# Two tiles of a shared expert moved: one behind the first attention projection, one into the first sums stage

## The chip, the cores and the metric

The kernel runs on one core of a Trainium2 chip. The metric is the device time of one execution in microseconds; a lower time is better. Time before: median 1554.01 us of three runs.

## What is computed

The reference is one block in three parts on x of 4 x 512 tokens, 512 wide, in float32:

```python
x = x + 0.5 * ffn(layernorm(x))        # router, 64 experts of 192, top 6, and a shared expert
x = x + attn(layernorm(x))             # 16 heads of 32, rope; attn adds its own input again
x = x + 0.5 * ffn(layernorm(x))
```

The shared expert is `silu(x @ ws_gate) * (x @ ws_up) @ ws_down`, for every token. In attn, scores of a head are 512 x 512, then softmax, then the product with the values, then the output projection.

## The kernel before, in words

Tokens are handled in 16 tiles of 128, four tiles to a batch (B = 4 batches, TPB = 4 tiles). The first feed-forward layer routes all tokens, computes the shared expert of the first three batches between the steps of the routing, and then runs the 64 routed experts (`experts`, L519), whose outputs are added into two arrays in HBM, `total[0][0]` and `total[0][1]`, by scattering DMAs from GpSimd (L576). Attention follows batch by batch, and the last feed-forward layer after it.

The join lies between the first experts and the attention (L1041 to L1053). There the shared expert of the fourth batch is still to be done; its four input tiles stay in SBUF in `xs[B - 1]`. For each tile it has these steps, all of class `Route`:

- `gate` (L477, by way of `gate_up`, L204): 4 matmuls of 128x384 on TensorE (gate and up together, L208), a tanh on ScalarE (L211), and, unless it is told to leave it out, `product`: two operations on VectorE (L214, L215).
- `turn_h` (L494): two transposes on TensorE (L201) and a copy on ScalarE to `hT` (L202).
- `down` (L502): two matmuls of 128x512 (L508), and an add into the tile of x on VectorE (L509).

The trace counts two TensorE records to each of these float32 matmuls and, for a transpose of this kind, one.

`load` (L603) brings each batch's tiles of x together: for batch 0 it loads the tile and a second operand, `odd`, on SyncE's queue (L608, L613), and the row adds them on VectorE (L786). For batches 1 and 2 it loads the tile and lets GpSimd accumulate the other array into it by DMA (L616); for batch 3 GpSimd accumulates both arrays into the tiles in SBUF.

`qkv(b)` (L780) gives the projections of a batch as a list of pieces, each with a cost written by hand: `row(0)` 0.1 and `turn(0)` 0.5, then for each tile `proj(i, 0)`, `proj(i, 1)`, `turn(i + 1)`, `proj(i, 2)` and two `heads`; a projection is marked 3.4. `row(i)` is a chain of some 18 operations on VectorE (add, statistics, reciprocal root by iteration, the layer norm itself at L799 and L800); `row(1)` is called inside `proj(0, 0)`, and the loads of batches 1 to 3 are issued inside `row(1)`. `turn` transposes the normed tile and copies it to `lT` on ScalarE. At the join the first batch's pieces run one after the other.

`sums(b, ...)` (L933) goes over the scores once to get maxima and sums. It has 16 rows (4 head groups c by 4 query tiles q). A row has its scores on TensorE (L965, two of three buffers of PSUM), two maxima on VectorE (L968) and four exponentials in place on ScalarE (L973). Pieces of other work are taken between, with these two methods of `Pieces`:

```python
    def short(self):

        if self.left and self.left[0][0] < 1.0:
            self.take()

    def long(self, keep=0):

        if sum(p[0] >= 1.0 for p in self.left) > keep:
            self.short()
            self.take()
```

A row issues its scores and maxima, then calls `short()`, then issues its exponentials, then calls `long(2)`. So a piece under 1.0 at the head of the list comes ahead of the row's exponentials, and a longer one behind them, and the last two long pieces are left for the end of the stage. In the first sums stage the list is the second batch's `qkv(1)`: with 12 projections, rows 1 to 10 take one each.

Each engine works its own queue in order. From the attention on, the order on TensorE, ScalarE and VectorE is the order in which the code issues; GpSimd's and SyncE's queues are ordered by the scheduler. The tile `sg` and the tile `hT` of the shared expert have one buffer each.

Of the kernel before, what the change touches and what calls it, by code (L numbers as in the profile page):

```python
# [18 lines left out]
B, S, D = 4, 512, 512  # L19
T = B * S  # L20
NT = T // P
TPB = S // P
# [61 lines left out]
def macaron_kernel(ctx: ExitStack, tc: tile.TileContext, X, ln_w, ln_b, W_in, W_out, gate_w, bias,  # L84
# [543 lines left out]
    with ExitStack() as s:  # L628
# [4 lines left out]
        with ExitStack() as f:  # L633
            rp = f.enter_context(tc.tile_pool(name="rp0", bufs=2))
            f.enter_context(tc.manual_schedule(engines={mybir.EngineType.SP}))
            xs = []
            for t in range(NT):
                g, i = divmod(t, TPB)
# [9 lines left out]
            route0 = route = Route(0)  # L648
# [4 lines left out]
            for t in range(2 * TPB + 1):  # L653
                g, i = divmod(t, TPB)
# [73 lines left out]
    with ExitStack() as s:  # L728
# [6 lines left out]
        psT = s.enter_context(tc.tile_pool(name="psT", bufs=2, space=bass.MemoryType.PSUM))  # L735
# [13 lines left out]
        xs, stats, qT, kT, v, nmT, keyed = xas, {}, {}, {}, {}, {}, {}  # L749
        work = Pieces()  # L750
# [103 lines left out]
        def project(b):  # L854
            mv = small.tile([P, TPB, 2], F32, tag="mv4", name="mv")

            def part(q):
                po = psT.tile([P, 512], F32, tag="ps", name="po")
                for c in range(NC):
                    nc.tensor.matmul(po, lhsT=qT[b][:, c, q * P:(q + 1) * P], rhs=win[3][:, c, :],  # L860
                                     start=c == 0, stop=c == NC - 1)
                nc.vector.tensor_add(xs[b][q], xs[b][q], po)
                if b < B - 1:
                    stat_later(b, mv, q)
                    if q == TPB - 1:
                        steps_later(route.ready(b, mv))
            return [(3.4, lambda q=q: part(q)) for q in range(TPB)]
# [173 lines left out]
        pieces, following = qkv(0), qkv(1)  # L1041
        pieces.insert(-2, following.pop(0))
        odds = [load(0, i, op) for i in range(2)]
        route0.use(rp, psT, Banks(), 1)
        for i in range(TPB + 1):
            if i < TPB:
                route0.gate(B - 1, i)
            if i == TPB:
                pieces.pop(0)[1]()
            if i > 0:  # L1050
                route0.turn_h(B - 1, i - 1)
                route0.down(B - 1, xs[B - 1], i - 1, False)
        nc.vector.memset(nmq, 0.0)  # L1053
        places(0)
        places(1)
# [2 lines left out]
        while work.left:  # L1058
# [2 lines left out]
            if done == len(pieces) // 3:  # L1061
                summed(1)
            work.flush(1)
        work.add(following)

        for ins in clear(1, range(NT + 1)):
            tc.add_manual_dep(ins, keyed[0].name, SENT, reason="behind the loads of the sums")
# [1 line left out]
        for b in range(B):  # L1069
            if b > 0:  # L1070
                pieces = project(b - 1)
                if b + 1 < B:
                    places(b + 1)
                    following = qkv(b + 1)
# [26 lines left out]
    with ExitStack() as s:  # L1101
# [6 lines left out]
        with ExitStack() as f:  # L1108
            g = B - 1
# [75 lines left out]
```

## Time and profile before

| what | value |
|---|---|
| timed runs | 1554.78, 1554.01, 1548.78 us; median 1554.01 |
| profiled execution | 1560.13 us |
| its span | 1558.4 us |
| mean granted TensorE clock | 0.946 |
| last expert's matmuls end (TensorE) | 451.0 us |
| shared expert of the fourth batch on TensorE | 452.41 to 474.35 us |
| first projection starts | 480.15 us |
| first sums stage: first scores, last scores | 532.98, 605.71 us |
| first scores of the context stage behind it | 617.51 us |

The profiled execution is one run; its span is from its first to its last instruction. In the rows of a timeline the columns are the start in us from the span's start, the duration in us, the engine (PE is TensorE, PEld its weight loads, DVE VectorE, ACT ScalarE, POOL GpSimd, SP SyncE), the line, the operation, what it writes and reads, shapes and the number of merged instructions, and in brackets the engine's idle time before it with what ended it. A row of the table of stretches has the stretch, its length, busy time and count for TensorE, its weight loads, VectorE, ScalarE and GpSimd, then the granted TensorE clock (1.00 is full), the busy share of the DMA engines and GB/s. On the page, the numbers behind an engine are its busy us, its share of the span and its instructions.

### The profile page before, as it was taken

What the parts mean: (1) busy time and instruction counts of PE and PEld (TensorE: products, weight loads), DVE (VectorE), ACT (ScalarE), POOL (GpSimd) and SP (SyncE); (2) the same over time, 40 slices, a digit from 0 to 9 for tenths busy, and PEclk for the clock granted to TensorE, in tenths of its full rate; (3) what the DMA queues carried; (4) which work ended last, traced back from release to release, by engine and by line L of the source; (5) the groups of instructions that cost most, each with busy time, mean ns of one, the idle gap of its engine ahead of it and who ended that gap; (6) DMA issues with size and microseconds to landing.
All of it is one profiled execution on the core that took longest, in us unless ns stands there. A gap on an engine that the chain in (4) does not pass through costs nothing.

```text
span 1558.4 us, 23015 instructions
## 1 busy us (share of the span) xinstructions
PE 1400.1 (90%) x9024; PEld 802.0 (51%) x9024; DVE 625.6 (40%) x1572; ACT 594.6 (38%) x1161; POOL 350.7 (23%) x321
## 2 busy tenths in 40 slices
PE   4785999999998998999999999988998799999990
PEld 4553777776753443333443434335334577777660
DVE  7575222211216575267245842375416422222210
ACT  4431121211111487668635774566452112121120
POOL 2001355554435000000000000000000245555535
PEclk9898899999999997999999999996898899999995
DMA  5477699999999300000000020000006389999989
GB/s 196 144 230 257 184 336 333 328 335 336 341 276 179 115 9 1 1 1 1 28 24 8 1 74 21 4 28 27 24 1 246 118 282 339 337 333 335 329 248 123
DMA packets 127035, 254.57 MB, mean 163 GB/s; under 512 B 15800, under 2 KB 32312, under 8 KB 126928
## 3 DMA queue, kind: packets, MB, share of 16 engines
q1 hardware_dynamic: 87216, 192.96, 35.2%
q0 software_dynamic: 39424, 59.97, 18.0%
q8 instruction: 72, 1.18, 0.3%
q14 instruction: 35, 0.29, 0.1%
q10 hardware_dynamic: 288, 0.16, 0.0%
HBM read 202.21 MB, written 56.95 MB: 166 GB/s over the span
## 4 chain that ended last, share of the span: by engine, by line
PE 56%; ACT 5%; DVE 4%; DMA 2%; issue 2%; POOL 1%; another core or an unknown queue 0%; POOLq 0%; SPq 0%; DVEq 0%; ACTq 0%
PE pq L811 10%; PE gu L549 6%; PE sct L995 5%; PE sc L965 4%; PE cx L1018 4%; PE sct L999 4%; PE ps_t L201 4%; PE eo L568 3%; PE po L860 3%; PE gu L208 3%; PE gu L553 2%; PE so L508 2%; PE eo L571 2%; ACT sc L973 2%; DMA w<-in_L_ffn_w_up_dram 1%
## 5 line engine op out<-in xcount | busy, mean ns | idle before, releaser
L526 POOL DMA_INDIRECT xr<-xn_d,en x128 | 119.5, 934 | 887.3 <-DVE sg L215 716.1
L549 PE MATMUL gu<-bT,w 128*128 128x96 f32 x2048 | 245.5, 278 | 8.3 <-DMA w<-in_L_ffn_w_up_dram 8.3
L549 PEld LDWEIGHTS gu<-bT,w 128*128 128x128 f32 x2048 | 238.5, 195 | 11.6 <-issue 11.5
L973 ACT ACTIVATE sc<-sc,nmq 128x512 f32<-128x512 f32 x256 | 168.9, 660 | 55.7 <-DVE nmq L968 50.0
L811 PE MATMUL pq<-w,lT 128*128 128x512 f32 x384 | 179.6, 615 | 6.6 <-ACT lT L202 2.7
L968 DVE TENSOR_REDUCE nmq<-sc 128x2 f32<-128x1024 f32 x128 | 151.5, 1221 | 74.0 <-PE sc L965 73.8
L576 POOL DMA_INDIRECT total<-ob,en x96 | 138.6, 1443 | 156.3 <-ACT ob L575 120.7
L575 ACT ACTIVATE ob<-eo,xr 96x512 f32<-96x512 f32 x128 | 80.5, 678 | 183.5 <-PE eo L571 180.2
L560 DVE SCALAR_TENSOR_TENSOR sg<-sg,gu 128x288 f32<-128x288 f32 x64 | 29.1, 454 | 301.7 <-ACT sg L559 224.0
L1006 ACT ACTIVATE pT<-sct 128x1024 f32<-128x1024 f32 x128 | 124.1, 1022 | 63.6 <-PE sct L999 63.6
L559 ACT ACTIVATE sg<-gu 128x288 f32<-128x288 f32 x64 | 26.2, 410 | 318.0 <-PE gu L555 318.0
L568 PE MATMUL eo<-w,hT 128*96 128x512 f32 x256 | 125.3, 612 | 0.0
L202 DVE COPY bT<-ps_t 128x384 f32<-128x384 f32 x128 | 65.7, 553 | 144.0 <-PE ps_t L201 121.1
L811 PEld LDWEIGHTS pq<-w,lT 128*128 128x128 f32 x384 | 71.6, 195 | 97.5 <-issue 80.9
L965 PE MATMUL sc<-kT,qT 32*128 32x512 f32 x512 | 93.8, 697 | 8.5 <-ACT sc L973 7.8
L555 PE MATMUL gu<-bT,w 128*64 128x96 f32 x1024 | 98.2, 249 | 0.0
L553 PE MATMUL gu<-bT,w 128*64 128x96 f32 x1024 | 98.2, 249 | 0.0
L995 PE MATMUL sct<-qT,kT 32*128 32x512 f32 x512 | 94.5, 658 | 2.3 <-ACT pT L1006 2.3
L208 PE MATMUL gu<-wsgu,xT 128*128 128x384 f32 x256 | 95.1, 519 | 1.4 <-ACT ob L575 1.4
L553 PEld LDWEIGHTS gu<-bT,w 128*64 128x64 f32 x1024 | 86.2, 137 | 6.0
L999 PE MATMUL sct<-nmT,pick 4*128 4x512 f32 x512 | 88.9, 612 | 0.0
L555 PEld LDWEIGHTS gu<-bT,w 128*64 128x64 f32 x1024 | 86.2, 137 | 0.0
(162 smaller groups left out, 1642.6 us busy)
## 6 DMA issues: line engine op xcount, KB each, us to landing
w<-in_L_ffn_w_gate_dram SPq DMA_DIRECT2D x64, 768.0 KB
w<-in_L_ffn_w_up_dram SPq DMA_DIRECT2D x64, 768.0 KB
w<-in_L_ffn_w_down_dram SPq DMA_DIRECT2D x64, 768.0 KB
total<-zero SPq DMA_DIRECT2D x39, 256.0 KB
xn_d<-xn SPq DMA_DIRECT2D x32, 256.0 KB
x<-in_L_attn_X_dram SPq DMA_DIRECT2D x16, 256.0 KB
x<-total POOLq DMA_DIRECT2D x16, 256.0 KB
out_dram<-x SPq DMA_DIRECT2D x16, 256.0 KB
```

Source lines behind the costliest of these rows:

```text
L208: nc.tensor.matmul(gu[:rows, :2 * F].rearrange("p (w f) -> p w f", w=2), lhsT=bT[:, c, :], rhs=weights[:, :, c, :], start=c == 0, stop=c = ...
L549: nc.tensor.matmul(g[:, k, :], lhsT=w[:, k, c, f:f + P], rhs=x[:, c, :], start=c == 0, stop=c == DC - 1)
L553: nc.tensor.matmul(g[:FC, 2, :], lhsT=w[:, 0, c, P:F], rhs=xa[:, c, :], start=c == 0, stop=c == DC - 1)
L555: nc.tensor.matmul(g[FC:, 2, :], lhsT=w[:, 1, c, 0:FC], rhs=xb[:, c, :], start=c == 0, stop=c == DC - 1)
L568: nc.tensor.matmul(eos[k][:CAP], lhsT=hT[:, k, :], rhs=wd[:, 2 * k, :], start=True, stop=False)
L576: nc.gpsimd.indirect_dma_start(out=total[layer][k], in_=ob, in_offset=None, out_offset=bass.IndirectOffsetOnAxis(ap=en[:, e:e + 1], axis=0 ...
L811: nc.tensor.matmul(pq, lhsT=lTs[i][:, c, :], rhs=win[n][:, c, :], start=c == 0, stop=c == DC - 1)
L965: nc.tensor.matmul(scs[j // 2][:, j % 2, :], lhsT=qT[b][rows, c, q * P:(q + 1) * P], rhs=kT[b][rows, c, :], start=True, stop=True)
L968: nc.vector.tensor_reduce(nmv[:, q, 2 * pair:2 * pair + 2, c], scs[pair], AX.X, ALU.max, negate=True)
L973: nc.scalar.activation(scs[j // 2][:, j % 2, :], scs[j // 2][:, j % 2, :], AF.Exp, bias=nmq[:, q, j * DH + c:j * DH + c + 1], accum_out=sm ...
L995: nc.tensor.matmul(scs[j // 2][:, j % 2, :], lhsT=kT[b][rows, c, kt * P:(kt + 1) * P], rhs=qT[b][rows, c, :], start=True, stop=False)
L999: nc.tensor.matmul(scs[j // 2][:, j % 2, :], lhsT=pick[rows, c, :], rhs=nmT[b][c // (NC - 1)][rows, :], start=False, stop=True)
```

## The change

At the join the loop over the four tiles is written out for three. The gates of tiles 0, 1 and 2 are issued, with tile 2's product left out for then; tiles 0 and 1 are turned and brought down. Then comes the first row's chain on VectorE (`pieces.pop(0)`), and behind it tile 2's product. Tile 2's turn and down are one piece of 1.7, put behind `proj(0, 0)`. Tile 3 becomes two long pieces in the list of the first sums stage, two entries ahead of its last projection: its gates with product (3.1), for which the PSUM pool is set to that of the transposes and projections, and its turn and down (1.7).

In the built program the order on TensorE changes in these places alone. The gates of tile 3 stand in row 10 of the first sums stage, its turn and down behind the scores of row 11 and ahead of those of row 12, and the projection that row 10 had stands behind the scores of row 12. On ScalarE the tanh of tile 3 comes ahead of row 11's exponentials, and the copy to `hT` behind them. On VectorE tile 3's product is ahead of row 11's maxima and its add ahead of row 12's. On GpSimd the accumulations into the tiles 2 and 3 of the fourth batch come first among those of L616 instead of last. Line numbers from the join on are higher by 12, and behind the first list of the sums stage by 13.

```diff
         route0.use(rp, psT, Banks(), 1)
-        for i in range(TPB + 1):
-            if i < TPB:
-                route0.gate(B - 1, i)
-            if i == TPB:
-                pieces.pop(0)[1]()
+
+        g, own = B - 1, xs[B - 1]
+        for i in range(3):
+            route0.gate(g, i, None if i < 2 else 1)
             if i > 0:
-                route0.turn_h(B - 1, i - 1)
-                route0.down(B - 1, xs[B - 1], i - 1, False)
+                route0.turn_h(g, i - 1)
+                route0.down(g, own, i - 1, False)
+        pieces.pop(0)[1]()
+        route0.product(g, 2)
+
+        def third():
+            route0.turn_h(g, 2)
+            route0.down(g, own, 2, False)
+
+        def fourth():
+            route0.turn_h(g, 3)
+            route0.down(g, own, 3, False)
+
+        pieces.insert(2, (1.7, third))
+        fourths = [(3.1, lambda: (setattr(route0, 'psM', psT), route0.gate(g, 3))), (1.7, fourth)]
...
-        work.add(following)
+        at = max(k for k, p in enumerate(following) if p[0] > 3.0)
+        work.add(following[:at - 2] + fourths + following[at - 2:])
```

## The prediction

> **What bounds the kernel now.** I read the page first, then the timeline of TensorE with VectorE from 440 to 535 us (the join of the first experts with the first attention row), then the timelines of TensorE, ScalarE and VectorE from 574 to 632 us (the end of the first sums stage), the granted clock in short windows, the moved bytes in 2 us windows, and how the changed program orders its instructions on each engine. On the page TensorE is busy 90% of the span and holds 56% of the chain that ended last:
>
> ```profile
> PE 1400.1 (90%) x9024; PEld 802.0 (51%) x9024; DVE 625.6 (40%) x1572; ACT 594.6 (38%) x1161; POOL 350.7 (23%) x321
> ```
>
> So a move can only win where TensorE idles. The join has such a place:
>
> ```profile
> 466.01 2.75 PE L208 MATMUL gu<-wsgu,xT 128*128 128x384 f32 x8
> ...
> 468.59 0.38 PE L201 MATMUL ps_t<-ident,sg 128*96 128x128 f32 x2
> ...
> 472.28 0.68 DVE L786 TENSOR_TENSOR x<-x,odd 128x512 f32<-128x512 f32 x1
> ...
> 477.54 0.75 DVE L800 SCALAR_TENSOR_TENSOR ln<-ln,rs,lnb_b 128x512 f32<-128x512 f32 x1
> ...
> 478.39 1.08 PE L201 MATMUL ps_t<-ident,ln 128*128 128x128 f32 x4 [4.04 <-issue]
> 480.15 9.16 PE L811 MATMUL pq<-w,lT 128*128 128x512 f32 x16 [0.67 <-ACT lT L202]
> ```
>
> VectorE adds the third tile's product at 471.67 and only then starts the first row's chain of small operations (472.28 to 478.29, 6.0 us). TensorE has finished the fourth tile's product by 474.35 and waits 4.04 us. From 480 to 586 us it runs with gaps of 0.25 to 0.7 us. Then the sums stage runs out of projections:
>
> ```profile
> 582.91 3.70 PE L811 MATMUL pq<-w,lT 128*128 128x512 f32 x8 [0.25 <-ACT qT L835]
> 586.54 1.99 PE L965 MATMUL sc<-kT,qT 32*128 32x512 f32 x12
> 590.61 1.13 PE L965 MATMUL sc<-kT,qT 32*128 32x512 f32 x4 [2.09 <-ACT sc L973]
> 592.09 1.13 PE L965 MATMUL sc<-kT,qT 32*128 32x512 f32 x4 [0.35 <-ACT sc L973]
> 594.20 8.71 PE L965 MATMUL sc<-kT,qT 32*128 32x512 f32 x20 [0.98 <-ACT sc L973]
> ```
>
> Numbering the sixteen rows of this stage by their scores (8 records each), row 10 has the last projection and rows 11 to 15 are paced by ScalarE's exponentials (L973), four to a row, 3.07 us with their accumulator reads. The first of rows 11, 12 and 13 start so:
>
> ```profile
> 588.97 0.66 ACT L973 ACTIVATE sc<-sc,nmq 128x512 f32<-128x512 f32 x1 [1.32 <-DVE nmq L968]
> ...
> 592.56 0.66 ACT L973 ACTIVATE sc<-sc,nmq 128x512 f32<-128x512 f32 x1 [0.52 <-DVE nmq L968]
> ...
> 595.53 0.65 ACT L973 ACTIVATE sc<-sc,nmq 128x512 f32<-128x512 f32 x1
> ```
>
> **The change, part by part.** No operation is added or dropped: the third tile's gates, product, turn and down and the fourth's are each issued once in both programs. SyncE's queue keeps its order.
>
> *Earlier first row.* VectorE now meets that chain right after the second tile's add, which ends at 466.90, if the two operands have landed. The hardware queue moved 0.49 MB from 462 to 464 and 0.47 MB from 464 to 466; the second operand is the third load of 0.262 MB, so its last bytes move near 465.3. The ninth load (2.36 MB) moved its last bytes near 471.4 and its waiter on GpSimd started at 473.58, 2.1 us later; by that measure the operand is there at 467.4. I take 467.4: 472.28 - 467.4 = 4.9 us earlier for everything that follows. Bounds: 466.9 (5.4) and 472.28, when it was used without a wait (0). What fell out of TensorE's queue was cover for this chain: it now idles from 466.2 to about 473.5, 7.3 instead of 4.04 us. Its clock then starts at half, as it did before (0.50 from 478 to 484), so the first projection costs the same.
>
> *Third tile behind the first projection.* Turn and down now lie between the two first projections. From the rows of before: turn 0.43, then ScalarE copies the projection (0.58) and only then hT, so the down starts about 1.0 after the projection's end (0.67 of waiting in the old place), and lasts 1.82. The second projection starts 2.8 to 3.1 later: +3.0 us. Its product (0.70) and the second row's chain on VectorE (5.7) lie beside 7 us of projection and cost nothing.
>
> *The add that now waits for DMA.* In the changed program GpSimd issues the accumulations into the third and fourth tiles first, ahead of the adds, so VectorE's add of the third tile (L509) waits for two of them. The first can go at 463.2; by the queue's progress (0.27 MB done by 472, sharing with the loads) it lands near 473.6, the second is issued then, and one alone takes some 5.7 us (issued near 495.6, its waiter on GpSimd starts at 501.30), 7.5 behind a full queue: there at 479 to 482. VectorE reaches the add near 484, when the down ends. Behind the add stand the rotation of the second projection (its copy comes at 488) and the third row's chain, with 3 us to spare. Cost 0; a landing after 491 would cost its lateness one for one. The second row batch's accumulations in the same queue go from 473.6 to about 478 to 488; their statistics are read from 490 on. Cost 0. One statistic moves ahead of the third row's chain, so the 0.45 us wait of the fourth turn (515.17) should go: -0.4.
>
> *Fourth tile in the sums stage.* Row 10 gets the gates (2.58) instead of the projection, row 11 turn and down, row 12 the projection. By busy time this looks free: TensorE idles some 9 us in rows 11 to 15, and ScalarE gets only 0.33 + 0.37. The order says otherwise. A row of the fourth batch's sums shows the gate's product ahead of a row's maxima:
>
> ```profile
> 1034.23 0.35 DVE L214 SCALAR_TENSOR_TENSOR sg<-sg,gu 128x192 f32<-128x192 f32 x1 [2.00 <-ACT sg L211]
> 1034.62 0.35 DVE L215 TENSOR_TENSOR sg<-sg,gu 128x192 f32<-128x192 f32 x1
> 1034.94 2.36 DVE L968 TENSOR_REDUCE nmq<-sc 128x2 f32<-128x1024 f32 x2
> ```
>
> In before's times: ScalarE is free for the tanh at 587.08, product at 587.44, row 11's maxima at 588.15 (587.71 before), its exponentials at +1.26, 589.4 to 592.5. There turn_h was a piece of its own, under 1.0, and taken ahead of the exponentials; here turn and down are one piece of 1.7, taken behind them. So hT is copied at 592.4, the down starts at 592.8, and row 12's scores stand behind it on TensorE. With a warm TensorE: down to 594.6, scores ready at 595.8, exponentials at 597.1 (592.56 before); the projection runs 595.7 to 599.3, then row 13's scores, and its exponentials start at 601.8 against 595.53: +6.2 us. From row 13 on both programs run alike.
>
> The clock decides the rest. It fell in this stage before:
>
> ```profile
> 586.00:590.00 4.00, 2.52 (x14) 0.69 (x12) 2.29 (x3) 2.65 (x6) 0.00 (x0) 1.00 0.00 0
> 590.00:594.00 4.00, 2.25 (x8) 0.60 (x8) 3.93 (x8) 3.41 (x10) 0.00 (x0) 0.94 0.00 0
> 594.00:598.00 4.00, 3.80 (x10) 1.51 (x12) 2.31 (x4) 3.45 (x11) 0.00 (x0) 0.50 0.00 0
> ```
>
> No gap on TensorE there was over 2.1 us, yet by 594 it stood at 0.50. In the changed order it does 0.4 us of work between 586.6 and 592.8, with one gap of 4.1 us. The Trainium skill ("TensorE: Matmul & The Clock Gate", Part 1, on the two states) puts the drop after at least one idle window of about 3.4 us, free-running: a gap of 4.1 us would cover a whole one only about one time in five, the sum would stay at 6.2. The row says that a half-busy TensorE is enough. I go by the row: down 3.45 and row 12's scores 2.1 at half clock (605.71 shows 2.09), the projection mostly warm again, 3.9; row 13's exponentials at 604.7, +9.2. A clock that stays warm a little longer in rows 14 and 15 gives back about 0.6. I take +8.6.
>
> Sum: -4.9 + 3.0 - 0.4 + 8.6 = +6.3 us. The profiled execution took 1560.13 us (span 1558.4), 6 above the median of the timed runs, 1554.01; I set the difference on the median: 1560.3.
>
> **The rivals.** *Hidden tail, not slower:* if row 12's scores didn't hang behind the down, the fourth tile would cost only ScalarE's 0.7: -4.9 + 3.0 - 0.4 + 0.7 = -1.6, 1552.4. For it speak the idle TensorE of rows 11 to 15; against it the order of the queues, in which hT's copy follows row 11's exponentials. It would need row 12's exponentials to start within about 1 us of their old distance from row 10. *The first row waits for its load:* if its operand lands as late as 472.28, the 4.9 are gone and TensorE has lost its cover: +3.0 - 0.4 + 8.6 = +11.2, 1565.2. For it: the loads share the engines with two accumulations that now come earlier; against it: 0.96 MB had moved by 466. It makes the change slower by over 0.5% from a landing near 469 on. *The add waits for its accumulations* past 491, some 10 us later than worked out: 5 us late would give 1565.
>
> **How the numbers follow.** Main case 0.62, its own range 1557.9 (warm, +3.9) to 1562.6 (cold, load a little late, +8.6); hidden tail 0.14; late load 0.16; the late add and what I don't see 0.08. The runs of before spread from 1548.78 to 1554.78, so the range is 1552 to 1567. Half a per cent (7.8 us) is about what a measurement of this kernel can tell from no change. Slower than 1561.8: a quarter of the main case, most of the late load, half of the rest, 0.33; faster than 1546.2: 0.03; within: 0.64.
>
> **What would show it.** Right: the first L811 about 5 us earlier against the end of the experts, the second projection 3 us behind the first; L202 of hT behind row 11's exponentials, a gap of some 4 us on TensorE ahead of that L508, a clock at 0.50 there, and the starts of rows 11's and 12's exponentials 10.2 us apart by the cold sum, 7.7 by the warm one (3.6 before). Wrong: L786 waiting for a load, L509 waiting for a DMA, or row 13's exponentials within 2 us of their old distance from row 10's.

## The result and the profile after

The changed kernel took 1571.01 us (median of six runs, 1562.23 to 1574.31) against 1551.39 for the kernel before (six runs beside it): a ratio of 1.0117, 95% interval 1.0095 to 1.0139. In a later, larger set the same kernel had 1567.85 us (twelve runs) against 1553.38, a ratio of 1.0074, 1.0050 to 1.0098. The ratios are taken over all runs of a set but the slow ones, those over 1.5% above the fastest of their kernel; they are not the quotients of the medians, which are 1.0126 and 1.0093. The forecast was 1560.3, with a range up to 1567. By the ratios the change costs 11 to 18 us, about twice to three times the 6.3 us forecast.

The profiled execution of the changed kernel took 1568.70 us, its span is 1567.0. First the join on TensorE, from its timeline; the experts end 0.9 us later than in the profile of before, which is to be taken off each start:

```profile
465.12 1.98 PE L508 MATMUL so<-wsd,hT 96*128 96x512 f32 x4 [0.67 <-ACT hT L202]
474.07 1.09 PE L201 MATMUL ps_t<-ident,ln 128*128 128x128 f32 x4 [6.97 <-issue]
475.83 6.00 PE L811 MATMUL pq<-w,lT 128*128 128x512 f32 x8 [0.67 <-ACT lT L202]
481.67 0.38 PE L201 MATMUL ps_t<-ident,sg 128*96 128x128 f32 x2
482.78 1.98 PE L508 MATMUL so<-wsd,hT 96*128 96x512 f32 x4 [0.72 <-ACT hT L202]
484.60 3.60 PE L811 MATMUL pq<-w,lT 128*128 128x512 f32 x8
```

The gap ahead of the first row has grown from 4.04 to 6.97 us, the first projection starts 5.2 us earlier against the experts (475.83 less 0.93, against 480.15), and the third tile lies between the two projections, 2.9 us of it. VectorE shows that neither DMA was waited for: the row's first add follows the second tile's add, and the third tile's add waited for TensorE:

```profile
467.14 0.69 DVE L509 SCALAR_TENSOR_TENSOR x<-so,x 128x512 f32<-128x512 f32 x1 [4.77 <-PE so L508]
467.95 0.69 DVE L786 TENSOR_TENSOR x<-x,odd 128x512 f32<-128x512 f32 x1
...
484.80 0.69 DVE L509 SCALAR_TENSOR_TENSOR x<-so,x 128x512 f32<-128x512 f32 x1 [0.89 <-PE so L508]
```

In rows 10 to 13 of the first sums stage TensorE did this:

```profile
584.49 1.14 PE L965 MATMUL sc<-kT,qT 32*128 32x512 f32 x8
587.13 0.40 PE L201 MATMUL ps_t<-ident,sg 128*96 128x128 f32 x2 [1.50 <-DVE sg L215]
591.52 3.78 PE L508 MATMUL so<-wsd,hT 96*128 96x512 f32 x4 [4.00 <-ACT hT L202]
595.24 1.77 PE L965 MATMUL sc<-kT,qT 32*128 32x512 f32 x8
596.93 3.70 PE L811 MATMUL pq<-w,lT 128*128 128x512 f32 x8
```

There is the gap of 4.00 us ahead of the fourth tile's down, and the down is twice as long as at full clock (3.78 for 1.98). The clock in that stretch, and row 12's scores, which start only at 595.24:

```profile
592.00:596.00 4.00, 4.00 (x8) 1.22 (x11) 0.66 (x1) 0.00 (x0) 0.00 (x0) 0.50 0.00 0
```

On ScalarE the first exponentials of rows 11, 12 and 13, the last one of row 11, and the copy to `hT` behind it. The transposes that the copy needs had ended at 587.53:

```profile
588.15 0.66 ACT L973 ACTIVATE sc<-sc,nmq 128x512 f32<-128x512 f32 x1 [1.95 <-DVE nmq L968]
...
590.44 0.66 ACT L973 ACTIVATE sc<-sc,nmq 128x512 f32<-128x512 f32 x1
...
591.12 0.35 ACT L202 COPY hT<-ps_t 96x256 f32<-96x256 f32 x1
598.31 0.66 ACT L973 ACTIVATE sc<-sc,nmq 128x512 f32<-128x512 f32 x1 [6.84 <-DVE nmq L968]
...
603.00 0.66 ACT L973 ACTIVATE sc<-sc,nmq 128x512 f32<-128x512 f32 x1 [1.15 <-DVE nmq L968]
```

Rows 11 and 12 are 10.16 us apart, against 3.59 before. I call this delay of rows 12 and 13 the late tail. The first scores of the first context stage come at 624.47, against 617.51. Counted from the start of the last matmul record of the first experts (451.36 and 450.43) that is 173.11 against 167.08: 6.03 us. The forecast for this place was 6.3.

So the join and the sums stage went as worked out, and the rest of the loss lies elsewhere. From here on the two programs issue the same work in the same order. I call the time from the first context scores to the start of the last experts' output matmuls the way; it has four parts, each from one context stage to the next, the last to those experts. The third part of the way, with a stretch of 41 us inside it, first in the changed kernel, then in before (columns as in the table of stretches):

```profile
933.09:1122.39 189.30, 176.04 (x795) 75.85 (x794) 82.23 (x177) 101.73 (x210) 0.00 (x0) 0.81 0.07 26
...
937.90:978.90 41.00, 41.00 (x168) 17.93 (x161) 5.46 (x21) 15.24 (x23) 0.00 (x0) 0.50 0.04 13
```

```profile
930.55:1107.60 177.05, 162.44 (x796) 71.46 (x795) 82.17 (x177) 101.43 (x210) 0.00 (x0) 0.89 0.07 27
...
934.00:975.00 41.00, 39.97 (x237) 17.80 (x236) 11.79 (x50) 20.81 (x31) 0.00 (x0) 0.92 0.05 21
```

The same 795 or 796 matmul records took 12 us longer. For 41.00 us the clock stood at 0.50, which I call half clock, while TensorE was busy all the time (41.00), and got through 168 records where before got through 237. This pair alone doesn't give the loss: the second and the fourth part are 4.4 and 6.9 us shorter in the changed kernel, so its whole way is 631.7 us against 630.8. The first profile of before was a long one, as two more will show.

### The profile page after: what moved, and what is told of

The parts are those of the page before. It is cut to its first block, busy times and chain, and to the rows that moved or that the text cites. A ratio compares the mean times of both kernels' runs of the same rounds, so it can differ in the third digit from the quotient of the medians.

```text
span 1567.0 us, 23007 instructions
## 1 busy us (share of the span) xinstructions
PE 1403.2 (90%) x9024; PEld 800.9 (51%) x9024; DVE 625.5 (40%) x1572; ACT 594.2 (38%) x1161; POOL 350.7 (22%) x321
## 4 chain that ended last, share of the span: by engine, by line
PE 53%; ACT 5%; DVE 4%; DMA 4%; issue 2%; POOL 1%; SPq 0%; POOLq 0%; ACTq 0%; DVEq 0%
PE pq L811 10%; PE gu L549 5%; PE sct L995 5%; PE cx L1018 4%; PE sc L965 4%; PE sct L999 4%; PE ps_t L201 3%; PE po L860 3%; PE gu L208 3%; DMA w<-in_L_ffn_w_up_dram 3%; PE eo L568 3%; PE so L508 3%; PE gu L553 2%; ACT sc L973 2%; PE eo L571 2%
## 5 line engine op out<-in xcount | busy, mean ns | idle before, releaser
L202 DVE COPY bT<-ps_t 128x384 f32<-128x384 f32 x128 | 65.6, 553 | 167.9 <-PE ps_t L201 167.8
```

## The experiments

Two theories went in. **Theory A:** the change itself costs 6 us, and the rest is time at half clock in later stages that differs from run to run. **Theory B:** the change sets that half clock off each time. A third, **A2**, came out of the first four runs: the clock changes in steps (every half-clock stretch in the traces is a multiple of 3.41 us, but for the last, which the end of the execution cuts off), and what a later stage loses depends on where it falls among the steps.

All ways and local times first, so that the runs can be read against one table. Local is the time from the last matmul of the first experts to the first context scores; each value of local and way is one profile. The clock is the mean granted clock of a whole execution, averaged over the timed runs that the ratio uses, and behind it that of before in the same set. The sets ran on three different chips: before took 1553.5 us on average in set 1, 1559.1 in set 2 and 1553.1 in set 3. So a total is compared only within its set.

| kernel | set | local, us | way, us | ratio to before (95%) | clock, before's |
|---|---|---|---|---|---|
| before, three profiles | | 167.1, 167.9, 167.0 | 630.8, 625.5, 622.4 | | |
| changed, two profiles | 1 | 173.1, 173.1 | 631.7, 631.7 | 1.0074 (1.0050 to 1.0098) | 0.939, 0.944 |
| sums part alone | 1 | 170.6 | 631.7 | 1.0061 (1.0023 to 1.0098) | 0.936, 0.944 |
| join part alone | 1 | 170.8 | 617.6 | 1.0034 (1.0012 to 1.0055) | 0.944, 0.944 |
| turn split off | 1 | 166.9 | 624.7 | 0.9991 (0.9971 to 1.0011) | 0.945, 0.944 |
| turn split off, again | 3 | 168.4 | 625.1 | 0.9985 (0.9959 to 1.0010) | 0.947, 0.943 |
| changed + 1 matmul | 2 | 173.4 | 632.5 | 1.0044 (1.0029 to 1.0059) | 0.943, 0.942 |
| changed + 2 matmuls | 2 | 173.5 | 628.6 | 1.0049 (1.0026 to 1.0072) | 0.943, 0.942 |
| changed + 4 in the stretch | 2 | 173.7 | 632.5 | 1.0062 (1.0046 to 1.0077) | 0.942, 0.942 |
| before + 2 matmuls | 2 | 167.0 | 639.2 | 1.0045 (1.0025 to 1.0066) | 0.938, 0.942 |
| better join | 3 | 166.7 | 625.2 | 1.0015 (0.9984 to 1.0045) | 0.942, 0.943 |

**The changed kernel again**, unedited.

> The changed kernel itself, once more, for the spread. In the one profile of it the first scores of the first context stage come 6.0 us later than before, counted from the end of the experts, and the timed runs are 18 us longer. Theory A: the change costs these 6 us, and the other 12 are time at half clock in later stages, which differs from run to run; then this profile has the same 6.0 within 1 us, half-clock stretches in other places than the first profile had, and a time between 1555 and 1575. Theory B: the change causes the 12 us too, by a half clock that it always sets off in the context stage of the third batch (about 938 to 979 us); then that stretch is there again, about 40 us long, and the time is 1568 to 1574.

Measured: local 173.1 again, way 631.7 again, the same stretch in the same place:

```profile
935.34:1124.66 189.32, 176.03 (x795) 75.80 (x795) 82.23 (x177) 101.81 (x210) 0.00 (x0) 0.81 0.07 26
...
940.10:981.10 41.00, 41.00 (x168) 17.95 (x161) 5.47 (x21) 15.30 (x23) 0.00 (x0) 0.50 0.04 13
```

The four parts were 138.76, 169.88, 189.32 and 133.78 us, all within 0.03 us of the first profile (138.76, 169.86, 189.30, 133.79). Theory A, that this is drawn anew each time, doesn't fit two profiles so alike. The twelve timed runs of this set still scatter from 1558.66 to 1571.52 us, and the stages of only one of them are on record, so the same place in every execution isn't shown.

**The turn as a piece of its own.**

```diff
-            route0.turn_h(g, 3)
             route0.down(g, own, 3, False)
...
-        fourths = [(3.1, ...), (1.7, fourth)]
+        fourths = [(3.1, ...), (0.3, lambda: route0.turn_h(g, 3)), (1.7, fourth)]
```

> The changed kernel with the fourth tile's turn as a piece of its own (0.3), so that the copy to hT stands ahead of row 11's exponentials. If the down behind hT is what makes the tail late (my step), row 12's exponentials start about 4 us after row 11's instead of 8 or more, TensorE has no gap of 4 us ahead of that L508, and the way from the experts' end to the context stage is about 5 to 6 us shorter than in the changed kernel, within 1 us of before. A rival, that the gates and maxima of row 10 and 11 make it late, leaves it within 1.5 us of the changed kernel. In the total: theory A 1546 to 1566, by the clock's luck; theory B (half clock set off by the late tail) as before, 1551.

Measured: local 166.9, 6.2 us less than the changed kernel and 0.2 less than before. TensorE's order is the same as in the changed kernel; only hT's copy has moved ahead of row 11's exponentials on ScalarE. The copy, and then TensorE:

```profile
587.33 0.37 ACT L202 COPY hT<-ps_t 96x256 f32<-96x256 f32 x1 [1.35 <-PE ps_t L201]
```

```profile
586.90 0.40 PE L201 MATMUL ps_t<-ident,sg 128*96 128x128 f32 x2 [1.50 <-DVE sg L215]
587.75 1.99 PE L508 MATMUL so<-wsd,hT 96*128 96x512 f32 x4 [0.46 <-ACT hT L202]
589.66 1.14 PE L965 MATMUL sc<-kT,qT 32*128 32x512 f32 x8
```

The gap of 4.00 us is 0.46, the down is at full clock, and row 12's exponentials start 4.2 us after row 11's (592.10 and 587.92). The tail's cost was this one copy behind four exponentials. The total is that of before, 1552.54 against 1553.38.

**The join's part alone**: the fourth tile's pieces behind the third's at the join.

```diff
-        pieces.insert(2, (1.7, third))
+        pieces[2:2] = [(1.7, third), (3.1, lambda: route0.gate(g, 3)), (1.7, fourth)]
...
-        work.add(following[:at - 2] + fourths + following[at - 2:])
+        work.add(following)
```

> The join's part alone: the third tile as in the changed kernel, the fourth tile's gates, turn and down directly behind it, ahead of the second projection; the first sums stage as before. Worked out: 4.9 earlier, 3.0 for the third tile, 7.1 for the fourth (2.6 of gates, 1.6 until its product, 0.4 turn, 0.7 until hT, 1.8 down), 0.4 given back: 4.8 us more than before up to the context stage, none of it in the sums. Theory B, if the late sums tail sets the later half clock off, has the total within 8 us of before; theory A anything from 1550 to 1570.

Measured: local +3.7 against the first profile of before (4.8 expected). Up to the first scores it was +4.7, as worked out, though the fourth tile took 6.7 us at the join and not 7.1; the sums stage, which was to stay as it was, took 83.5 us and not 84.5, and I don't know why. The stretch of 41 us is gone, and the way is the shortest seen, 617.6. That is no typical way of this kernel, for the profiled execution (1543.47 us) was the fastest of its 22 timed runs, whose median is 1560.22. In the timed runs +0.34%.

**The sums stage's part alone**: at the join only three tiles are issued, with the first row's chain at the place where it was (`if i == 3`, ahead of the last turn); the two pieces of the fourth tile as in the changed kernel.

```diff
-        for i in range(TPB + 1):
-            if i < TPB:
+        for i in range(4):
+            if i < 3:
...
-            if i == TPB:
+            if i == 3:
```

> The sums stage's part alone: the join as before for three tiles, without the fourth; its two pieces in rows 10 and 11 as in the changed kernel. The first row starts 2.7 earlier (the third product's add is that much earlier), and rows 10 to 13 are late by the same 8 to 9 us as in the changed kernel: +5 to +6 us up to the context stage. If the late rows came of the third tile's move, the tail would be as before and the total 3 us shorter. In the total theory B has 1568 to 1574 again, theory A 1552 to 1572.

Measured: local +3.5 (5 to 6 expected). The first projection started 5.7 us earlier and not 2.7: in my edit the chain stands ahead of the third tile's add, which I had overlooked. From the first scores to the context stage it took 92.75 us, the changed kernel 92.68, before 84.53: the late tail is 8.2 us in both, and the third tile's move has no part in it. Behind it the way was 631.7 with the same four parts (138.77, 169.87, 189.31, 133.79): in this profile the late tail alone brings the long half clock with it. The median of the ten timed runs, 1567.13 us, lies just under theory B's range and inside theory A's. The mean clock speaks for B: 0.936 here and 0.939 in the changed kernel, and 0.944 to 0.945 in the kernels of the same set that have no late tail.

**Shifted by half a step and by a quarter.** Two matmuls, or one, into a tile that nothing reads, ahead of the second batch's sums:

```diff
         for b in range(B):
+            for _ in range(2 if b == 1 else 0):
+                nc.tensor.matmul(psT.tile([P, 512], F32, tag="ps", name="idle"), lhsT=ident,
+                                 rhs=win[3][:, 0, :], start=True, stop=True)
```

> The changed kernel with two matmuls more (identity by a slice of W_out, into a tile that nothing reads) ahead of the second batch's sums stage, where TensorE is the bound: 2 x 0.86 = 1.7 us of added work, which also moves everything behind it by half of the 3.4 us in which the granted clock steps. In three profiles with the late tail the way from the first context stage to the last experts takes 631.7 us each time, with the same 41 and 31 us at half clock; with the tail mended or left alone it takes 617.6 to 630.8. Theory A2: these losses come of where the stages fall among the steps of the clock, and the late tail put them there; then 1.7 us more work changes the way by more than itself, some 5 to 12 us less, and the total falls below the changed kernel's 1568 in spite of the work. Rival: the losses belong to what the changed kernel issues in these stages; then the way is 633.4 and the total 1.7 longer.

> As the last, with one matmul more (0.86 us, a quarter of a step). Theory A2: the two long half-clock stretches change place or length, the way from the first context stage to the last experts differs from 631.7 + 0.9 by over 3 us. Rival: 632.6, and the total 0.9 longer than the changed kernel's 1568.

Measured, two matmuls: way 628.6, which is 3.1 less than in the profiles of the changed kernel, without the added 1.7 us of work; the saving expected (5 to 12) was too large, the sign right. The parts are 142.4, 169.9, 175.3 and 141.0: the third is 14 us shorter and the fourth 7 longer. The first grew by 3.6 us, with a new half-clock step near its end, so the later stages were moved by a whole step and not by half of one. One matmul: way 632.5 with parts 139.8, 172.6, 177.1 and 142.9; the stretch of 41 us is gone here too, but the sum is no different from 631.7 + 0.9, so by my own criterion for the sum this run speaks for the rival, by the criterion of place for A2. A shift of a microsecond or two goes with up to 14 us moved from one stage to another.

The totals, 1566.88 and 1565.90 us, can't be held against the 1568 of set 1, for before itself took 1558.77 here. Within the set they are 7.6 and 6.9 us above before by the ratios, which is the local 6.0 and the added work of 1.7 and 0.9, with no mean clock lost (0.943 against 0.942). So here the loss behind the tail is gone, as A2 has it. The changed kernel without added matmuls was not run on this chip; whether the shift or the chip took the loss away is not shown.

**Before, shifted by the same two matmuls.**

> The kernel before with the same two matmuls more as in the shifted changed kernel: 1.7 us of work. Theory A2: before is by luck of place on a good spot (its timed runs have their mode at 1553 to 1555), so a shift of half a step costs more than 1.7 or changes little: 1553 to 1565, and the half-clock stretches behind the first context stage stand elsewhere. Rival: 1555.1, the stretches where they were.

Measured: 1567.41 us against 1558.77, by the ratio +0.45%, some 7 us for 1.7 us of work, and a mean clock of 0.938 against 0.942. The total lies above the 1553 to 1565 expected, but before itself is 5 us slower in this set than in set 1. A half clock of 37.5 us stands in the second part of the way now, where no profile of before has one over 7 us:

```profile
764.10:801.60 37.50, 37.50 (x154) 16.60 (x153) 4.89 (x18) 14.88 (x21) 0.00 (x0) 0.50 0.04 15
```

So the long half clock needs nothing of the changed kernel: before falls into it too. The added work is not all that moved it there. In this profile a half-clock step at 620.7 us, ahead of the added matmuls (668.4) and in no profile of before, had already cost some 1.7 us; with the work the second part starts 3.6 us later than in before (142.3 against 138.8 us behind the first context scores), a whole step. No profile of before itself was taken on this chip.

**Four matmuls of full height inside the stretch**, in the third step of the third batch's context stage (`(c, kt) == (0, 2)`, b = 2), otherwise the changed kernel.

> The changed kernel with four matmuls of full height more in the third step of the third batch's context stage, in the half-clock stretch (3.4 us at full clock, 6.9 at half; nothing reads them). If the stretch lasts 41 us because the matmuls of this stage, of 32 and of 4 rows, never look busy enough to the clock, full-height work ends it one or two steps later: the stretch is 7 to 14 us instead of 41, and the way through this stage 5 to 9 us shorter in spite of the added work. If the clock only counts time in which TensorE is busy (it was busy throughout there), they change nothing but their own 3.4 to 6.9 us.

Measured, TensorE's timeline around them (behind the operands stand rows*columns of the array that a matmul uses):

```profile
944.41 2.09 PE L995 MATMUL sct<-qT,kT 32*128 32x512 f32 x8
946.27 1.93 PE L999 MATMUL sct<-nmT,pick 4*128 4x512 f32 x8
948.13 6.66 PE L1029 MATMUL idle<-w,ident 128*128 128x512 f32 x8
954.63 0.60 PE L201 MATMUL ps_t<-ident,xn 128*128 128x128 f32 x4
955.16 1.07 PE L1018 MATMUL cx<-pT,v 128*32 128x512 f32 x8
```

The half clock ended with them, after 17.1 us instead of 41, and the third part took 185.1 us instead of 189.3, with 6.7 us of work added. Both sizes miss what was expected (7 to 14 us of half clock, 5 to 9 us saved), the direction is right. The unedited changed kernel agrees: its stretch ended at 978.9 us, 2.4 us into the stage's own first gate matmuls, which use 128 rows too, and the stretch in before with two matmuls ended 2.3 us into the first gates of its stage.

```profile
976.47 4.01 PE L208 MATMUL gu<-wsgu,xT 128*128 128x384 f32 x8
```

So a few long matmuls of full height in a row ended the half clock, and the mixed work ahead of them did not. Whether their height, their width or their following each other counts, no run separates. Nor is such a row always needed: in the first profile of before the same stage left its half clock after 6.8 us (934.8 to 941.6 us) with mixed work alone. The shorter stretch brought nothing in the end: the fourth part took 138.8 instead of 133.8, and by its ratio, 1.0062, the total is no different from the changed kernel's 1.0074 within the intervals. The four matmuls are 3.4 us of work at full clock, and the total stands 9.7 us above before: about the local 6.0 and that work.

**Before, twice more, for its profile.**

> The kernel before, once more, for its profile alone. The first profile of it has 630.8 us from the first context stage to the last experts at a time of 1560.1, 6 above its timed runs. If the changed kernel's excess over its 6 us is lost behind the first context stage, a typical execution of before needs some 624 us there (630.8 less the 6 to 7 that this execution lay above the median), and this profile shows 618 to 628, with 60 to 82 us at half clock on that way. If it shows 630 or more again, the excess is lost elsewhere, ahead of the join or in the last experts.

> The same once more: 618 to 628 us on that way by the theory, 630 or more against it.

Measured: 1555.60 and 1549.71 us, ways 625.5 and 622.4. Both as the theory had it, with 75 and 72 us at half clock. The first profile of before, at 630.8, is the longest of the three.

**The split turn again, and a better join.**

> The kernel with the fourth tile's turn as a piece of its own, once more. The way from the experts' end to the first context stage is 166.9 again within 0.6 us. Behind it: if a kernel has its own place among the clock's steps, 624.7 and the same stretches at half clock as in its first profile; if the place is drawn anew in each execution, others. Total within 0.4% of before.

> A better join: the gates of the third and the fourth tile both ahead of the first row's chain, both products behind it, the third tile's turn ahead of the first projection, in the gap of the copy to lT, and the fourth's turn and both downs behind that projection; the sums stage as before. Worked out against before, up to the first context stage: 5.3 earlier (as measured in the changed kernel), 0.2 for the turn, 0.4 + 1.8 + 1.8 for the turn and the downs, 0.45 given back: -1.4 us. TensorE's gap ahead of the first row shrinks from 7.0 to 4.4 us. In the total 1.4 us less is within what the clock adds or takes: within 0.5% of before, better if the place is good.

```diff
+        route0.last = True
+        route0.gate(g, 3, 1)
+        route0.last = False
         pieces.pop(0)[1]()
         route0.product(g, 2)
+        route0.product(g, 3)
+        pieces.insert(1, (0.3, lambda: route0.turn_h(g, 2)))
...
+        pieces.insert(3, (3.4, both))
```

Here `both` is the fourth tile's turn with the two downs. Measured, split again: way 625.1, but with other half-clock stretches than in its first profile, and 1.5 us more ahead of it (168.4), so it has no fixed place, and its local time missed the 166.9 expected. Better join: local 166.7, 0.4 less than before where 1.4 was expected: the row's first add waited 1.34 us for its load, and the early turn held the first projection until its product was there (first projection 4.0 us earlier, not 5.3). Neither differs from before in the timed runs.

## Why the prediction was wrong

The step that failed is *"From row 13 on both programs run alike"*, which put everything behind the first sums stage at nothing. It holds for the order of the work and for the rest of that stage. It doesn't hold for the clock: kernels with the late tail spent more of the later stages at half clock, and the way of the changed kernel was 5.5 us longer than that of before. By its steps, against the experts' end:

- *Earlier first row, -4.9:* -5.2. Right; the load was there in time. *"The first projection costs the same":* nearly; it took 5.8 us up to the next work and not 5.6, with 4.7 us of it at half clock against 4.1.
- *Third tile, +3.0:* +2.9. *The add behind two accumulations, 0:* no wait for them. *The fourth turn's wait, -0.4:* it is gone, but a wait of 0.28 us for a copy stands behind that turn now, and the gain is 0.1. First scores of the sums stage -2.1 (80.43 against 82.55), -2.3 forecast.
- *Fourth tile in the sums stage, +8.6:* +8.15. The mechanism is shown by the split turn, which takes all of it away. The choice between row and rule on the clock was right: the down ran at half clock. It fell to half at 589.7 us, at the end of a step of 3.41 us in which the trace has 0.40 us of TensorE work.
- *Sum +6.3:* 6.03 up to the first context scores, and no large errors that cancel.
- *"From row 13 on both programs run alike", 0:* The way took 631.7 us in all three profiles with the late tail and nothing else changed behind it (95.6 us at half clock each). In the three profiles of before it took 626.2 on average (72 to 79 us at half clock). That is 5.5 us more, and with the local 6.0 it makes 11.5, the excess by the ratio 1.0074. In all seven profiles without the tail and without added work the average is 624.5; it leans on the join part's fastest run.
- *The same in the timed runs:* over the twelve of the changed kernel 95.4 us of full clock were not granted on average (one less the mean clock, times the span), over the 52 of before beside them 87.6. Where two runs of before differ by 1 us in that, they differ by 0.45 us in time, so I estimate 3.5 us for the 7.8, or 4.7 at the 0.6 of the runs of the split turn and the sums part. The three-by-three comparison and this estimate are both rough.
- What the first six runs (1.0117, 18 us) have above it isn't explained. The parts outside the local time and the way add up to 753 to 764 us in these profiles, and scatter with work that the change doesn't touch; in the two profiles of the changed kernel they are 3.1 us longer than in the three of before.
- Of the prediction's rivals, none gave this. The late load and the late add didn't come; the tail wasn't hidden.

Taking the runs of before as they scatter (1543 to 1565 in 52 runs of one set), I had read their spread as noise about one profile. It is in part time at half clock: between a run's time and the clock it was not granted the correlation is 0.55 to 0.80 in the three sets of before. A change that moves the rest of the program moves that too.

What is shown: the late tail costs 8.2 us and comes of hT's copy; with it, in set 1, the mean clock falls from 0.944 to 0.939 and 0.936, and splitting the turn brings clock and total back to before's; a long half clock comes in before too, in a profile in which it is moved by a step; four matmuls of full height ended one early. What is only argued: why the late tail ties the program to one place among the steps. In all six profiles with it the steps lie at the same distance from the first context scores, within 0.1 us (half clock from 34.7 and from 17.7 us ahead of them), while in before they lie up to 0.25 us apart and with the split turn 0.7. A stage that starts at half clock and is released by a step ends nearer to the step than it began, which would do it; no run tested that. And why the stretch lasts: at half clock one step of the context stage's loop takes 8.54 us (its transposes start at 940.44, 948.98 and 957.52 in the changed kernel), which is two and a half steps of the clock, so in every second pass the clock's steps fall on the same work again. Whether that keeps it at half is not shown either.

## What to carry to other kernels

A wait that is small for its engine can hold another's queue: ask not only who is idle but behind what the copy in between stands, and in which order a planner puts a piece that is made of two steps. In a kernel whose granted clock goes to half and back in its stages, a local sum, however exact, gives the local part only; compare the granted clock stage by stage, in several profiles of each kernel, before a total is read as the worth of an edit. Look where a profiled run stands among the timed ones, and compare totals on one chip.

## What the runs showed of the hardware

Full busy time alone does not bring the clock back. In the context stage TensorE was busy, by its records, for 41.00 of 41.00 us at 0.50, with matmuls on 4, 32 and 128 rows in turn; 6.7 us of long matmuls on all 128 rows ended the same stretch. The Trainium skill ("TensorE: Matmul & The Clock Gate", Part 1, the table of the two states) gives full clock after at least one busy window of about 3.4 us; the stretches here are multiples of 3.41 us, which agrees with the window, but twelve such windows without a gap did not release it, and here the measurement decides. And the clock fell to half without a whole idle window: in the sums stage of before, at 593.5 us, the 3.41 us ahead of the fall hold 2.3 us of TensorE work, and no gap in the rows there is over 2.1 us.
